# Four graph layers on one core: softmax scores spread by a DRAM round trip, with a new order of the work

## The chip, the core and the metric

The kernel runs on one core of a Trainium2 chip. A core has a matrix engine, TensorE (PE in the profile; PEld is its loading of weights), a vector engine, VectorE (DVE), a scalar engine, ScalarE (ACT), a general engine, GpSimd (POOL), and SyncE (SP), which here issues every DMA. Each engine runs its own instructions strictly in order and waits on semaphores. SBUF is the on-chip memory of 128 partitions; PSUM is the memory that matmuls write, here used as 8 banks of 128 x 512 floats.

The metric is the device time in microseconds (us) of one launch that handles all 64 graphs.

## The reference

64 graphs of 256 nodes with 512 features go through four layers. Each layer normalizes the features, applies relu, and adds the layer's result to the features:

```python
h = jnp.maximum(_layernorm(x, axis=-1), 0.0)
x = x + _L0_gnn_ref(h, adj, L0_gnn_W_qk, L0_gnn_W_v)
```

Layers 1 (attention with 8 heads, masked by the adjacency) and 2 (8 heads, tanh of masked scores) are not touched except in their place in time. Layers 0 and 3 give each node one score and take a softmax over the 256 nodes of its graph. Layer 0:

```python
scores = jnp.einsum('bnd,bmd->bnm', q, k) * inv_scale
w = jnp.sum(scores * adj_matrix, axis=-1, keepdims=True)
w = jax.nn.softmax(w, axis=1)
return w * v
```

Layer 3 does the same with other projections: `w` from `q` and `adj @ k`, a softmax over nodes, then `w * v`. Everything is float32.

## The kernel before

**Tiling.** Every tile has 128 partitions; a graph's 256 nodes are two nodes per partition (`c` = 0, 1). A loop over 64 graphs (b) is written out whole. The work of one graph is cut into 150 named steps, each a function that issues a few instructions, nearly always on one engine. A name ends in its layer or part:

- `load` (SP): features, adjacency, and the adjacency once more as 32 x 32 blocks (tile `blocks`). `at` (DVE) transposes the blocks; `neg`, `negt` (ACT) make additive masks.
- per layer: `st` (DVE statistics), `rs` (DVE), `pw` (POOL, power -0.5), `sh` (DVE, shift), `hn` (ACT, normalized relu), `sq` (DVE, block transposes), `sw` (SP, store to a DRAM tile `sq_d`), `ht` (SP, four reads that complete the transposition). PE multiplies `ht` with weights.
- layer 0: `qk` and `qe` (PE, ACT), `score0` (PE), `s0v` (DVE: one score per node, tile `wc`, 128 x 2).
- layer 1: `fa`, `fb` (PE projections), `fae`, `fbe` (DVE), `send`, `er`, `enes` (per-node terms to DRAM and back to all partitions, 2 MB), `max` (DVE), `mxv`, `mxt`, `mr`, `mb` (maxima to DRAM and back to all partitions, 1 MB), `ea`, `ex` (ACT), `eg`, `eh` (POOL), `eb` (DVE), `po`, `su`, `sp` (PE), `se`, `oe` (ACT), `sr` (DVE), `sqo`, `swo`, `or`, `oa` (result through DRAM, then POOL adds it).
- layer 2: `xp`, `xe`, `sqx`, `swx`, `xpt`, `xc`, `xcv`, `xca`, `ps`, `tv`, `ta`, `py`, `ye`, `sqy`, `swy`, `yr`, `yg`, `yv`.
- layer 3: `agg`, `ga`, `z`, `zv` (scores into `wc`), `am`.
- the softmax over nodes, in layers 0 and 3, built by `weighted`: `pv` (PE, the values), `softp` (PE), `softv` (DVE, maximum), `softa` (ACT, exponentials and their sum), `softw` (DVE, weights of the node pairs), `add` (DVE, adds weighted values to the features). `store` (SP) ends the graph.

`softp` is the step that the change replaces. Each partition holds two scores, but the maximum and the sum run over all 256. Two PE transposes of a broadcast column (line 751 in the profile) put all 256 scores on every partition, in a PSUM bank. Line 756 is `softv`, 761 and 763 are `softa`, 768 and 769 `softw`, 775 `add`.

**Order.** Nothing schedules at run time. Tables give every step a number: `WEIGHTS` for set-up, `FIRST` for the first six graphs, `LAST` for the last five, `TIMES` for all others, and graph b's numbers are shifted by b times `PERIOD`. All steps of all graphs are sorted by that number, and the five engines' instructions are pinned in the sorted order:

```python
steps += [(b * PERIOD + at, b, name) for name, at in times.items()]
```

So up to five graphs are in flight, and each engine takes turns among them. The numbers are keys for sorting; no engine waits for a clock.

**Buffers.** `keep(kind, count, ...)` makes a fixed number of tiles of a kind. `take` pops the oldest free one, `done` gives it back, both in the sorted order, so the order also decides who waits for whose buffer. Every DMA is issued by SP, in order: a step whose wait isn't over holds up all DMAs behind it.

**Lines used below.** 639 is every projection from `ht` (`qk`, `pv`, `fa`, `fb`, `xp`, `z`); 650 the `ht` reads; 733 the `sq_d` stores; 706 `sh`; 701 `pw`; 942 `eg`; 966 `po`; 896 `max`; 1149 `yg` and `yv`; 645 `sq`.

## Time and profile before

| What | Value |
|---|---|
| median of 3 runs | 3910.57 us (3908.46 to 3915.72) |
| time of the profiled execution | 3894.62 us |
| its span, first to last instruction | 3892.8 us |
| instructions in the span | 52870 |
| matmuls of the removed step (line 751) | 256, 53.4 us busy |
| all DMA | 784.71 MB, mean 202 GB/s |
| share of 16 DMA engines' span, data queue | 63.8% |

The page gives for each engine its busy time, its share of the span and its number of instructions. A stretch is a part of the span, with the same per engine. A wait line names the waiting engine and line, what it waited for, the total in us, how often, and the longest. A group line gives busy time, mean length of one in ns, and the engine's idle time ahead of it. A timeline line gives start, length, engine, line, operation, and in brackets the idle time before it and what ended it. The chain is followed back from the last instruction through whatever released each step.

### The profile page before, as it was taken

The numbers are of one execution on the slowest core, as the hardware profiler recorded it, in microseconds if no ns is written. First come the engines' busy times: TensorE is split into PE (matmuls) and PEld (weight loads), VectorE is DVE, ScalarE is ACT, GpSimd is POOL, SyncE is SP. The second block draws the span as 40 slices with busy tenths as digits, with TensorE's granted clock in tenths as the row PEclk, the third lists the DMA queues.
The fourth block names the chain that finished last, engine by engine and source line by source line (L and its number), as shares of the span: only waits on it lengthen the run. The fifth ranks groups of instructions, "written<-read, shape, count | busy, mean of one in ns | idle before, by whom it ended". The sixth has DMA issues, their size and how long they took to land.

```text
span 3892.8 us, 52870 instructions
## 1 busy us (share of the span) xinstructions
PE 3677.6 (94%) x16322; PEld 2126.0 (55%) x16322; DVE 3060.4 (79%) x7449; ACT 1872.2 (48%) x3653; POOL 1531.4 (39%) x1229
## 2 busy tenths in 40 slices
PE   6789999999999999999999999999999999999889
PEld 3455555555555555555555555555555555555544
DVE  5777787887888787787787787887788787787784
ACT  2444554545545544545544544545545544544442
POOL 1434343444344344343344344343344344344341
PEclk9899999999999999999999999999999999999999
DMA  7565666666666666666666666666666666666553
GB/s 200 168 193 179 208 200 212 214 203 213 216 201 211 217 200 212 207 199 207 215 195 213 207 202 214 214 204 209 216 201 216 214 198 215 209 200 196 181 182 103
DMA packets 967435, 784.71 MB, mean 202 GB/s; under 512 B 788913, under 2 KB 859121, under 8 KB 942577
## 3 DMA queue, kind: packets, MB, share of 16 engines
q1 hardware_dynamic: 967152, 781.34, 63.8%
q8 instruction: 130, 2.13, 0.2%
q14 instruction: 153, 1.25, 0.1%
HBM read 511.12 MB, written 270.01 MB: 201 GB/s over the span
## 4 chain that ended last, share of the span: by engine, by line
PE 46%; DVE 20%; DMA 17%; SPq 8%; issue 5%; POOL 3%; ACT 2%; DVEq 0%; ACTq 0%; POOLq 0%
PE bank L639 34%; DVE sq L645 7%; DMA ht<-sq_d 6%; SPq L650 5%; DMA sq_d<-sq 5%; PE bank L1111 4%; PE bank L966 3%; DVE pair L948 2%; DVE junk L896 2%; DMA hn<-sq_d 2%; PE bank L1097 2%; DVE stats L690 2%; DMA blocks<-in_adj_dram 2%; DVE xt L775 2%; DVE shift L706 1%
## 5 line engine op out<-in xcount | busy, mean ns | idle before, releaser
L639 PE MATMUL bank<-w_s,ht 128*128 128x256 f32 (+2 forms) x3072 | 965.7, 462 | 80.7 <-DMA ht<-sq_d 69.0
L639 PE MATMUL bank<-wv_s,ht 128*128 128x512 f32 x2048 | 906.3, 594 | 0.0
L639 PEld LDWEIGHTS bank<-w_s,ht 128*128 128x128 f32 x3072 | 587.4, 198 | 381.3 <-issue 288.2
L713 ACT ACTIVATE hn<-xt,shift,rstd 128x512 f32<-128x512 f32 x512 | 388.7, 806 | 828.8 <-DVE shift L706 759.5
L942 POOL TENSOR_TENSOR pair<-pair,negt 128x1024 f32<-128x1024 f32 x256 | 604.5, 2374 | 117.2 <-ACT pair L935 117.2
L639 PEld LDWEIGHTS bank<-wv_s,ht 128*128 128x128 f32 x2048 | 397.3, 197 | 444.8 <-issue 442.8
L975 POOL TENSOR_TENSOR half<-pair 128x512 f32<-128x512 f32 x256 | 331.3, 1306 | 593.1 <-PE bank L989 328.0
L896 DVE CUSTOM_DVE_ANT_0 junk<-all,adj 128x256 f32<-128x256 f32 x1024 | 472.8, 462 | 31.4 <-issue 0.2
L639 PE MATMUL bank<-m_s,ht 128*128 128x512 f32 x1024 | 455.5, 597 | 8.2 <-DMA ht<-sq_d 6.8
L935 ACT ACTIVATE pair<-all,ec 128x256 f32<-128x256 f32 x1024 | 433.4, 497 | 9.8 <-DMA all<-er_d 9.8
L1149 POOL TENSOR_TENSOR xt<-xt,hn 128x512 f32<-128x512 f32 x64 | 111.4, 1741 | 811.7 <-DMA hn<-sq_d 811.7
L690 DVE BATCH_NORM_STATS2 stats<-xt 128x6 f32<-128x512 f32 x512 | 332.3, 680 | 96.3 <-POOL xt L1034 88.5
L701 POOL TENSOR_TENSOR rstd<-rstd,power 128x2 f32<-128x2 f32 x256 | 179.5, 702 | 407.0 <-DVE rstd L697 390.9
L645 DVE STREAM_TRANSPOSE sq<-hn 128x512 f32<-128x512 f32 x512 | 331.8, 686 | 5.0 <-ACT hn L713 4.9
L966 PE MATMUL bank<-pair,feats 128*64 128x256 f32 x2048 | 272.4, 401 | 62.2 <-ACT pair L954 62.0
L1129 DVE TENSOR_TENSOR pair<-bank,at 128x512 f32<-128x512 f32 x512 | 317.0, 669 | 12.2 <-PE bank L1097 12.0
L954 ACT ACTIVATE pair<-pair 128x1024 f32<-128x1024 f32 x256 | 264.0, 1050 | 118.4 <-DVE pair L948 111.2
L639 PEld LDWEIGHTS bank<-m_s,ht 128*128 128x128 f32 x1024 | 197.2, 198 | 221.4 <-issue 216.4
L948 DVE TENSOR_TENSOR pair<-pair,all 128x1024 f32<-128x1024 f32 x256 | 303.4, 1223 | 15.3 <-DMA all<-m_d 14.4
L1032 POOL TENSOR_TENSOR hn<-hn,rs 128x256 f32<-128x256 f32 x256 | 152.3, 617 | 392.4 <-DMA hn<-sq_d 317.7
L761 ACT ACTIVATE bank<-bank,nmax 128x256 f32<-128x256 f32 x128 | 56.8, 443 | 504.5 <-DVE nmax L756 504.5
L1136 ACT ACTIVATE pair<-pair 128x512 f32<-128x512 f32 x512 | 285.8, 617 | 16.1 <-DVE pair L1129 16.0
(83 smaller groups left out, 4541.8 us busy)
## 6 DMA issues: line engine op xcount, KB each, us to landing
sq_d<-sq SPq DMA_DIRECT2D x448, 512.0 KB
ht<-sq_d SPq DMA_DIRECT2D x1024, 128.0 KB
all<-er_d SPq DMA_DIRECT2D x128, 1024.0 KB
all<-m_d SPq DMA_DIRECT2D x64, 1024.0 KB
hn<-sq_d SPq DMA_DIRECT2D x512, 128.0 KB
xt<-in_x_dram SPq DMA_DIRECT2D x64, 512.0 KB
xpt<-sq_d SPq DMA_DIRECT2D x256, 128.0 KB
out_dram<-xt SPq DMA_DIRECT2D x64, 512.0 KB
```

What stands on the lines that cost most here:

```text
L639: nc.tensor.matmul(p, chunk(ht[:, k], c), w[:, k], start=(k == 0), stop=(k == KC - 1))
L645: nc.vector.transpose(sq.rearrange("p (r k i c) -> p c k r i", r=4, k=KC, c=NC)[:, c], t[:, c])
L690: nc.vector.bn_stats(stats[:, c, :], g["xt"][:, c, :])
L713: nc.scalar.activation(hn[:, c, :], g["xt"][:, c, :], AF.Relu, bias=st["shift"][:, c:c + 1], scale=st["rstd"][:, c:c + 1])
L896: nc.vector.tensor_tensor_reduce(junk, g["en"][:, h, :], g["adj"][:, c, :], 1.0, -BIG, OP.add, OP.max, g["mx"][:, c, h:h + 1])
L935: nc.scalar.activation(e[:, s, j, :], g["es"][:, h, :], AF.Prelu, bias=st["ec"][:, j, H + h:H + h + 1], alpha=0.2)
L942: nc.gpsimd.tensor_tensor(e, e, g["negt"][:, None].to_broadcast([P, 2, NC, N]), OP.add)
L948: nc.vector.tensor_tensor(e, e, g["m"][:, 2 * p:2 * p + 2, None, :].to_broadcast([P, 2, NC, N]), OP.subtract)
L966: nc.tensor.matmul(po[s * U:(s + 1) * U, p % 2, :], feats[:, j, h * U:(h + 1) * U], e[:, s, j, :], start=(j == 0), stop=(j == NC - 1))
L975: nc.gpsimd.tensor_tensor(g.take("half", name=f"h{p}"), e[:, :, 0, :], e[:, :, 1, :], OP.add)
L1129: nc.vector.tensor_tensor(th[:, s], g[f"ps{p}{s}"].rearrange("p (m n) -> p m n", m=NC), g["at"], OP.mult)
L1136: nc.scalar.activation(g[f"th{p}"][:, s], g[f"th{p}"][:, s], AF.Tanh)
```

## The change

The step `softp` goes. In its place stand `ws`, which stores the 128 x 2 scores to a DRAM tile `w_d`, and `wb`, which reads them back as one row of 256 to all 128 partitions, into an SBUF tile of a new kind `pr` (two of them). `softv` and `softa` then read that SBUF tile and no PSUM bank. The kind `blocks` has one tile in place of two. In the set-up the names of two banks get the number of their part. All tables have new numbers, and `PERIOD` is 57.0; 152 steps a graph.

```diff
@@ -471,13 +473,14 @@
     keep("hn", 2, [P, NC, D])
     keep("ht", 3, [P, KC, N])
     keep("sq", 2, [P, NC * D])
-    keep("blocks", 2, [P, N // S, S * NC])
+    keep("blocks", 1, [P, N // S, S * NC])
     keep("feats", 2, [P, NC, D])
     keep("cols", 2, [P, KC, N])
     keep("all", 3, [P, H, N])
     keep("pair", 4, [P, 2, NC, N])
     keep("negt", 2, [P, NC, N])
     keep("qk", 2, [P, NC, 2 * A0])
+    keep("pr", 2, [P, N])
     keep("mx", 1, [P, NC, S])
     keep("half", 2, [P, 2, N])
 
@@ -594,7 +597,7 @@
             @step(f"mt{e}")
             def _():
                 for s in range(2):
-                    pt = g.take("bank", name=f"wt{s}")
+                    pt = g.take("bank", name=f"wt{s}{e}")
                     for k in range(KC):
                         nc.tensor.transpose(pt[:, k * P:(k + 1) * P], st[f"wn{e}"][:, s, k], ident)
 
@@ -602,10 +605,10 @@
             def _():
                 st["w_t"] = w_t = once.tile([P, 2, D], F32, name="w_t", bufs=1)
                 nc.vector.tensor_copy(w_t[:, 0, :].rearrange("p (k d r) -> p k d r", k=KC, r=4),
-                                      g["wt0"].rearrange("p (k r d) -> p k d r", k=KC, r=4))
-                nc.vector.tensor_copy(w_t[:, 1, :], g["wt1"])
-                g.done("wt0")
-                g.done("wt1")
+                                      g[f"wt0{e}"].rearrange("p (k r d) -> p k d r", k=KC, r=4))
+                nc.vector.tensor_copy(w_t[:, 1, :], g[f"wt1{e}"])
+                g.done(f"wt0{e}")
+                g.done(f"wt1{e}")
 
             @step(f"mm{e}")
             def _():
@@ -744,21 +747,24 @@
                 value(c)
 
 
-            @step(f"softp{layer}")
-            def _():
-                pr = g.take("bank", name="pr")
-                for c in range(NC):
-                    nc.tensor.transpose(pr[:, c * P:(c + 1) * P], st["wc"][:, c:c + 1].to_broadcast([P, P]), ident)
+            @step(f"ws{layer}")
+            def _():
+                st["w_d"] = rows_d.tile([P, NC], F32, name="w_d")
+                nc.sync.dma_start(st["w_d"], st["wc"])
+
+            @step(f"wb{layer}")
+            def _():
+                nc.sync.dma_start(g.take("pr"), st["w_d"].rearrange("p c -> (p c)").partition_broadcast(P))
 
             @step(f"softv{layer}")
             def _():
                 st["nmax"] = small.tile([P, 1], F32, name="nmax")
-                nc.vector.tensor_reduce(st["nmax"], g["pr"][:, :N], AX.X, OP.max, negate=True)
+                nc.vector.tensor_reduce(st["nmax"], g["pr"], AX.X, OP.max, negate=True)
 
             @step(f"softa{layer}")
             def _():
                 st["tot"] = small.tile([P, 1], F32, name="tot")
-                nc.scalar.activation(g["pr"][:, :N], g["pr"][:, :N], AF.Exp, bias=st["nmax"], accum_out=st["tot"])
+                nc.scalar.activation(g["pr"], g["pr"], AF.Exp, bias=st["nmax"], accum_out=st["tot"])
                 st["w"] = small.tile([P, NC], F32, name="w")
                 nc.scalar.activation(st["w"], st["wc"], AF.Exp, bias=st["nmax"])
                 g.done("pr")
```

The tables of the middle graphs, old and new (`WEIGHTS`, `FIRST` and `LAST` are changed as thoroughly):

```diff
-PERIOD = 59.0
+PERIOD = 57.0
 TIMES = {
-    "load": 0.000, "st0": 8.598, "at": 14.291, "rs0": 17.770, "pw0": 18.151, "sh0": 19.827, "hn0": 20.197,
-    "sq0": 22.027, "neg": 23.076, "sw0": 23.619, "ht0": 26.810, "negt": 33.560, "qk0": 36.920, "qk1": 37.838,
-    "qe0": 38.562, "qe1": 39.097, "score0": 39.117, "s0v": 42.489, "softp0": 45.404, "softv0": 48.091,
-    "softa0": 48.731, "pv00": 49.189, "softw0": 52.829, "pv01": 53.476, "add0": 56.587, "st1": 58.282,
-    "rs1": 60.040, "pw1": 60.420, "sh1": 61.401, "hn1": 61.771, "sq1": 63.601, "sw1": 65.193, "ht1": 68.384,
-    "fa1": 73.209, "fa0": 75.198, "fae0": 77.504, "fae1": 78.257, "send": 79.376, "er": 79.818, "enes": 83.628,
-    "max0": 93.041, "ea0": 93.130, "ea1": 95.760, "max2": 97.616, "fb0": 97.757, "max1": 97.783, "max3": 99.552,
-    "mxv": 102.131, "mxt": 103.746, "ea2": 104.173, "mr": 104.189, "eg1": 105.093, "mb": 107.595, "ea3": 108.549,
-    "eg0": 108.704, "eb0": 112.651, "eb1": 113.945, "ex0": 114.332, "eg2": 115.240, "ex1": 115.461, "eh1": 117.705,
-    "fb1": 118.902, "fbe0": 119.237, "eg3": 120.587, "fbe1": 121.996, "po0": 122.625, "po1": 123.961,
-    "eb2": 124.009, "ex2": 125.487, "eb3": 125.789, "eh0": 126.598, "ex3": 126.782, "po2": 127.022, "oe0": 127.910,
-    "su0": 128.127, "po3": 128.638, "eh3": 128.740, "oe1": 129.974, "eh2": 130.055, "sqo": 130.841, "su1": 131.698,
-    "se": 132.525, "swo": 132.976, "or": 132.996, "sp": 136.188, "sr": 138.013, "oa0": 139.860, "oa1": 142.480,
-    "st2": 145.314, "rs2": 147.072, "pw2": 147.452, "sh2": 148.433, "hn2": 148.803, "sq2": 150.633, "sw2": 152.225,
-    "ht2": 155.416, "xp0": 159.864, "xp1": 163.649, "xe0": 166.754, "xe1": 167.673, "sqx": 168.592, "swx": 171.012,
-    "xpt": 174.204, "xc": 179.698, "xcv": 181.830, "ps0": 183.981, "tv0": 187.172, "xca": 187.563, "ps1": 188.658,
-    "ta0": 189.627, "tv3": 192.016, "tv1": 193.393, "tv2": 197.635, "ta1": 198.812, "ta3": 200.645, "ta2": 201.909,
-    "py0": 202.513, "ye0": 202.533, "py1": 204.554, "ye1": 206.911, "sqy": 207.777, "swy": 211.577, "am": 212.932,
-    "yr": 217.212, "yv": 221.001, "yg": 221.746, "st3": 223.517, "rs3": 225.557, "pw3": 225.938, "sh3": 230.347,
-    "hn3": 230.717, "agg1": 233.270, "agg0": 235.086, "sq3": 238.587, "sw3": 240.179, "ga0": 241.452,
-    "ga1": 242.287, "ht3": 248.180, "z0": 254.433, "z1": 257.973, "zv0": 258.289, "zv1": 261.830,
-    "softp3": 265.594, "pv31": 265.839, "softv3": 268.089, "softa3": 268.742, "pv30": 269.380, "softw3": 274.098,
-    "add3": 280.909, "store": 282.605,
+    "load": 0.000, "st0": 0.020, "rs0": 0.040, "pw0": 0.060, "sh0": 0.447, "hn0": 0.467, "at": 3.235, "sq0": 4.046,
+    "neg": 5.196, "sw0": 7.794, "ht0": 17.081, "negt": 24.877, "qk1": 25.097, "qk0": 25.928, "qe0": 26.481,
+    "pv01": 26.487, "qe1": 26.501, "score0": 26.521, "s0v": 30.777, "ws0": 30.797, "wb0": 34.828, "softv0": 36.256,
+    "softa0": 36.276, "pv00": 41.031, "softw0": 42.595, "add0": 46.118, "st1": 47.198, "rs1": 47.218,
+    "pw1": 47.238, "sh1": 48.261, "hn1": 48.281, "sq1": 50.408, "sw1": 57.622, "ht1": 58.705, "fa0": 58.725,
+    "fae0": 61.292, "fa1": 62.955, "fae1": 64.080, "send": 64.100, "er": 65.670, "enes": 68.954, "max0": 78.054,
+    "max2": 80.041, "max1": 80.835, "ea2": 81.782, "max3": 81.811, "ea0": 82.877, "mxv": 86.226, "mxt": 87.431,
+    "fb1": 87.694, "mr": 88.442, "fbe1": 92.928, "mb": 92.952, "ea1": 93.137, "eg0": 97.342, "eg2": 97.898,
+    "eb2": 99.758, "fb0": 101.023, "eg1": 102.751, "ex2": 103.007, "fbe0": 104.462, "ea3": 105.281, "eb0": 106.770,
+    "po2": 107.965, "ex0": 109.416, "eg3": 110.046, "po0": 110.200, "eb1": 110.242, "ex1": 110.262, "eb3": 112.539,
+    "ex3": 112.559, "eh0": 112.721, "po1": 113.101, "po3": 113.362, "oe0": 113.726, "oe1": 113.772, "eh1": 114.964,
+    "su0": 114.984, "sqo": 116.823, "swo": 116.843, "or": 116.985, "eh2": 121.455, "eh3": 121.545, "su1": 121.565,
+    "se": 121.585, "sp": 124.333, "sr": 124.353, "oa1": 127.236, "oa0": 132.559, "st2": 132.579, "rs2": 132.599,
+    "pw2": 132.619, "sh2": 133.501, "hn2": 135.131, "sq2": 135.151, "sw2": 137.255, "ht2": 140.479, "xp0": 146.490,
+    "xp1": 148.494, "xe0": 150.546, "xe1": 153.892, "sqx": 155.064, "swx": 156.419, "xpt": 161.348, "xc": 167.559,
+    "xcv": 170.132, "ps0": 171.632, "tv1": 175.365, "xca": 177.302, "ps1": 179.802, "ta1": 179.832, "tv0": 180.487,
+    "tv2": 182.563, "ta0": 182.818, "py0": 182.838, "ta2": 182.910, "tv3": 184.557, "ta3": 184.577, "am": 184.723,
+    "ye0": 185.950, "py1": 187.683, "ye1": 187.703, "sqy": 190.038, "swy": 190.249, "yr": 195.562, "yv": 200.772,
+    "yg": 202.748, "st3": 203.788, "rs3": 205.029, "pw3": 205.049, "sh3": 206.251, "hn3": 206.271, "sq3": 210.021,
+    "sw3": 210.041, "agg1": 212.553, "ht3": 213.760, "agg0": 218.026, "ga0": 222.008, "z0": 223.305,
+    "zv0": 228.215, "ga1": 229.617, "z1": 239.253, "zv1": 242.471, "ws3": 243.288, "pv30": 245.126, "wb3": 249.737,
+    "pv31": 252.572, "softv3": 255.150, "softa3": 256.059, "softw3": 260.763, "add3": 262.405, "store": 266.901,
 }
```

Sorted, the new order of the middle graphs is, from one `load` to the next (steps of several graphs in flight):

- PE: ps0, su0, fa0, fa1, su1, ps1, sp, z1, py0, py1, pv30, pv31, qk1, qk0, pv01, score0, fb1, xp0, xp1, pv00, agg1, fb0, agg0, po2, z0, po0, xc, po1, po3.
- DVE: st0, rs0, zv0, sh0, sqo, at, sq0, fae0, tv1, fae1, send, tv0, sr, tv2, tv3, zv1, st2, rs2, sqy, sh2, max0, sq2, max2, max1, max3, softv3, mxv, yv, mxt, s0v, softw3, st3, rs3, add3, sh3, fbe1, softv0, xe0, sq3, xe1, sqx, softw0, eb2, add0, st1, rs1, fbe0, sh1, eb0, sq1, eb1, eb3.
- POOL: pw0, eh1, eh2, eh3, oa1, oa0, pw2, yg, pw3, eg0, eg2, eg1, pw1, eg3, eh0.
- SP: load, sw1, ht1, swo, or, sw0, er, enes, ws3, ht0, swy, wb3, sw2, yr, ht2, ws0, mr, wb0, mb, store, sw3, swx, ht3, xpt.

## The prediction

> **What bounds the kernel now.** I read the page's busy shares first, then the chain that ended last (its part 4), then the waits of TensorE.
>
> ```profile
> PE 3677.6 (94%) x16322; PEld 2126.0 (55%) x16322; DVE 3060.4 (79%) x7449; ACT 1872.2 (48%) x3653; POOL 1531.4 (39%) x1229
> ...
> PE 46%; DVE 20%; DMA 17%; SPq 8%; issue 5%; POOL 3%; ACT 2%; DVEq 0%; ACTq 0%; POOLq 0%
> ```
>
> TensorE (PE) is nearly full, yet under half of the chain is PE: the rest goes through VectorE (DVE) and DMA round trips that finish just in time. The stretches give the size of the leftover:
>
> ```profile
> 400.00:800.00 400.00, 388.21 (x1743) 224.53 (x1742) 319.75 (x799) 201.00 (x395) 160.85 (x129) 1.00 0.66 207
> 800.00:1600.00 800.00, 777.27 (x3525) 453.54 (x3524) 645.30 (x1605) 401.69 (x788) 323.56 (x261) 1.00 0.67 210
> 1600.00:2400.00 800.00, 768.84 (x3462) 447.11 (x3461) 640.29 (x1567) 394.54 (x768) 327.39 (x259) 1.00 0.65 206
> 2400.00:3200.00 800.00, 780.62 (x3508) 453.03 (x3506) 647.15 (x1607) 404.31 (x792) 330.48 (x264) 1.00 0.66 210
> ```
>
> The first pair of numbers after the length is PE busy. A graph has 254 PE instructions, so these 2800 us hold 12238/254 = 48.2 graphs: 58.1 us each, PE busy 56.35, idle 1.77. What that idle waits for:
>
> ```profile
> PE bank L639 <- DMA ht<-sq_d: 94.6, 87, 12.4
> PE bank L966 <- ACT pair L954: 62.0, 57, 8.8
> ```
>
> Projections wait for transposed activations from DRAM; `po` waits for the exponentials. Why these are late is seen in the timeline of one graph (start, length, engine):
>
> ```profile
> 1910.85 0.70 POOL L701 TENSOR_TENSOR rstd<-rstd,power 128x2 f32<-128x2 f32 x1 [0.42 <-DVE rstd L697]
> ...
> 1911.52 2.35 POOL L942 TENSOR_TENSOR pair<-pair,negt 128x1024 f32<-128x1024 f32 x1
> 1911.59 2.30 DVE L706 SCALAR_TENSOR_TENSOR shift<-mv,rstd 128x2 f32<-128x2 f32 x1 [0.49 <-POOL rstd L701]
> ```
>
> A tiny `sh1` takes 2.30 us because GpSimd (POOL) starts `eg3` just before it; elsewhere it takes 0.16.
>
> **What the skill says.** (1) "SBUF — State Buffer", section on the two sides: DVE and GpSimd share a port pair as an exclusive lock for a whole instruction, taken also by a DVE operation with two SBUF inputs. The lines above agree: 2.30 against 0.16. (2) "DMA: Bandwidth & Descriptors", anatomy of one DMA: a fixed cost of about 2.0 us, mostly the receipt of the write. The trace agrees: its chain has a 512 KB `sq_d<-sq` at 2.64 us and `ht<-sq_d` at 2.79. (3) Same page, specifications: pieces under 512 B are below line rate. The new store has 8-byte pieces; no row of before shows them. (4) "Perfetto Trace Analysis", most-contended engine: matmul busy share misleads, as matmuls are pipelined. So I price PE by spacing of starts.
>
> **The change, part by part.** Durations below are from start to next start in the middle graphs' timelines.
>
> Removed: two transposes in each of two softmaxes. In
>
> ```profile
> 2056.74 0.43 PE L751 MATMUL bank<-ident,wc 128*128 128x128 f32 x2
> 2057.01 4.46 PE L639 MATMUL bank<-wv_s,ht 128*128 128x512 f32 x10
> ```
>
> a pair holds PE for 0.27 us, in the other layer 0.22: 0.49 per graph. The group's busy time gives an upper end, 53.4/64 = 0.83. I take 0.49 (31 us in 64 graphs); PE's floor is 56.35 - 0.49 = 55.86 per graph.
>
> Added: `ws` and `wb`, twice per graph. Each issue costs SP 0.35 us (like `sw`), 1.4 per graph; SP issues about 24 us of work per graph, so it has room, but it waits in order. Landing: `ws` 2 to 4 us (nearest: `er_d<-er` 1.8 to 2.7, `sq_d<-sq` 2.6, by semaphore updates in the trace), `wb` about 2.8 (like a 128 KB `ht` piece). So one `ws`+`wb` trip is 5 to 7 us in place of 0.5. Layer 0: its user add0 wants pv00, which PE ends 12 us after score0 (fb1, xp0, xp1, pv00: 1.73+3.52+3.44+3.43), so PE hides it; but DVE is in order, and between s0v and softv0 it has only softw3 to fbe1, 5.4 us in the loop below. At 6.1 (0.35+2.6+0.35+2.8) softv0 stands 0.7 late, of which 0.5 reaches xe1; bounds 0 and 2. Behind `wb0` on SP wait `mb`, then store; `mb` has m_d's own landing to wait for anyway. Layer 3: `ws3` stands between `enes` and `ht0` and waits for zv1; behind it `ht0`, `swy`, `wb3`. Counted from the start F of fa0: z1 ends at F+10.0, zv1 10.8, `ht0` issued 11.2 to 14.1, its last piece landing 5.9 later by the same place of before (behind the 2 MB `enes`): 19.3. qk1 wants it at 20.4. Hidden, slack 1.1. `wb3` lands near 20, softv3 stands at 24: slack 4.
>
> softv and softa read SBUF instead of PSUM: no row shows it; PSUM costs 0.39 and 0.45 us, I take no difference (0.1 either way, on engines with room). Two bank uses per graph go, 0 to a small gain. One `blocks` tile less: `load` of a graph now follows `at` of the previous by 135 steps, almost a period; nothing, and 3 us of SP per graph if `at` ran that late. The `wt` names only rename set-up banks: nothing.
>
> Moved: the whole order, the main term. The tightest loop of the new order, from F to the next F:
> - PE fa0, fa1, su1, ps1, sp, z1, py0, py1: 1.83+1.92+0.57+1.94+0.23+3.44+1.78+1.83 = 13.6 with the end of the last; ye1 0.65: 14.3.
> - DVE sqy 1.17, sh2 0.08, max0 1.71, sq2 1.21: 18.5. Then max2, max1, max3, softv3 5.8: 24.3. Meanwhile `swy` lands at 19.2 and `yr` at 23.8, POOL runs `yg` 1.75 to 25.6, and mxv (two SBUF inputs) is locked out until then.
> - mxv, yv, mxt, s0v, softw3, st3, rs3: 0.75+0.61+0.16+0.54+0.40+1.41+0.15 = 4.0: 29.6. pw3 0.75, then `eg0` starts at once, 2.35: sh3 locked until 32.7 (add3 runs beside).
> - hn3 and sq3's second half 2.3: 35.1. xe1 wants xp1, which PE ends at 35.4: 36.0. sqx, softw0, eb2, add0, st1, rs1: 2.07+0.40+1.13+1.32+1.41+0.15 = 6.5: 42.5.
> - pw1 0.75, `eg3` locks sh1 2.35: 45.6. hn1's half and eb0: 46.9; sq1 1.21: 48.1. `sw1` and `ht1` to fa0: 7.85 in before (8.35 in the graph shown): 55.9 to 56.4, or 56.9 with the 0.5 of softv0.
>
> So loop and PE floor lie within 1 us, near 56; three lock stalls (1.3, 1.8, 2.2) are inside. po0 wants ex0 about 0.4 after PE is there. Before has three such near-ties (fa1 0.32, xp0 0.66, po2 0.57 idle, medians) and so 1.77 idle. In the new order I count fa0, po0 and qk1, each at 0.3 to 0.5: idle 1.1, period 57.0. Saving 1.1 per graph; 54 graphs are steady (3130 us between 400 and 3530): 60 us. Filling: `ws0`/`wb0` of the first graphs hold SP while weights wait behind, 5 us lost, between -10 and +20; the end has pv31 of 61 and both pv of 63 (10.3 us) over the last trip, nothing. Sum -55. The profiled run took 3894.6 with a span of 3892.8; the median 3910.57 is 16 higher for the same work, so I put the difference on the median: 3856.
>
> **Rivals.**
> R1, the waits vanish: period 55.9 to 56.3, saving 97 to 119, time 3795 to 3815. For: loop and floor are nearly equal. Against: in the steady stretch before never ran below 57.4, with idle 0.9 to 1.1 even then.
> R2, the gain is eaten by the three locks and by landings behind `load`: `sw1` is issued 1.3 us after `load` instead of 4.4, so its 2.6 us may become 3.5. PE idle 2.0 to 2.4, time 3890 to 3920.
> R3, slower: `ws3` at the head of SP. It is in order, so if zv1 or the landing behind `enes` is late, `ht0` is, and qk1 stalls PE, each us in full. Slack is 1.1, the gain before it is 2.25 (58.11 - 55.86): beyond 3.3 us later than reckoned the kernel is slower. At 4 to 5 late it is +0.7 to +1.7 per graph, +40 to +90: about 3970. For: `hn` and `ht` waits are already PE's largest, and `ht0` lands at 6.6 instead of 2.8 when behind `enes`. Against: zv1 has its input at 10.0 and DVE is free by 9.2.
>
> **How the numbers follow.** The main case (3835 to 3880) gets 0.45; R1 0.17; R2 0.18, half of it faster and a third the same; R3 0.20. About 0.2% (8 us) is what a measurement can tell from no change. Faster: 0.45+0.17+0.09 = 0.71, as 0.70; same 0.06; slower 0.24. The range leaves out the lower end of R1 and most of R3: 3797 to 3930.
>
> **What would show it.** Right: no L751; PE busy near 55.9 per graph and period near 57; sh1 and sh3 at about 2 us; mxv late behind `yg`; softv waiting nowhere long for a DMA. Wrong: a large wait of DVE softv for `pr<-w_d`, or of PE qk for `ht<-sq_d` with SP held at the w_d store (R3); PE idle over 2 with fa0 waiting (R2); filling longer than 20 us more. It would also be wrong if DVE and POOL meet in other pairs than those named.

## The result, and the profile after

The changed kernel takes 4137.55 us (median of 4, 4134.67 to 4145.81) against 3913.14 (3908.46 to 3916.34) for the kernel before, measured together: a ratio of 1.0578, 95% interval 1.0557 to 1.0599. I had said 3856 with a range of 3797 to 3930. The sign is wrong and the time is far outside. The profiled executions say the same: 4134.67 against 3894.62.

The page of the changed kernel, part 1 (busy time, share of the span, instructions):

```profile
PE 3752.1 (91%) x16066; PEld 2107.1 (51%) x16066; DVE 3196.0 (77%) x7449; ACT 1906.5 (46%) x3653; POOL 1544.0 (37%) x1229
```

The 256 transposes are gone (16322 to 16066 instructions), and yet PE is busy for longer and has a smaller share of a longer span. The stretches of the changed kernel, with the columns as before:

```profile
400.00:800.00 400.00, 365.07 (x1503) 203.81 (x1502) 302.12 (x717) 179.04 (x347) 138.76 (x111) 0.97 0.69 193
800.00:1600.00 800.00, 758.95 (x3309) 427.33 (x3307) 651.23 (x1519) 392.01 (x749) 316.35 (x250) 0.98 0.73 203
1600.00:2400.00 800.00, 744.36 (x3230) 418.70 (x3226) 641.38 (x1508) 385.16 (x739) 311.73 (x247) 0.99 0.73 201
2400.00:3200.00 800.00, 742.06 (x3214) 416.12 (x3210) 634.71 (x1496) 380.89 (x734) 308.80 (x245) 0.99 0.73 199
```

A graph now has 250 PE instructions, so 11256/250 = 45.0 graphs in 2800 us: 62.2 us each, PE busy 2610.4/45.0 = 58.0, idle 4.2. Before it was 58.1, 56.35 and 1.77; I had forecast 57.0 with 1.1 idle. (A stretch doesn't hold whole graphs, so this count is good to some 0.3 us. Taken from `fa0` to `fa0` over graphs 15 to 50, counted from 0, the changed kernel has 61.7 with 57.7 busy and before 58.3 with 56.5.) The waits of the changed kernel, over all engines (engine, line, tile, what it waited for, total us, times, longest):

```profile
DVE nmax L762 <- DMA pr<-w_d: 230.4, 74, 11.7
...
PE bank L642 <- DMA ht<-sq_d: 145.2, 109, 6.8
...
PE bank L972 <- DVE feats L871: 94.3, 50, 2.7
```

Line 762 is `softv` (756 before): DVE stands 230 us for the score rows, a wait that did not exist. Line 642 is the projections (639 before): 145 against 94.6. Line 972 is `po` (966 before): it no longer waits mostly for exponentials but for `feats`, which DVE writes in `fbe0`, a step that stands behind `softv0` in DVE's order.

Where they come from is seen in one graph. SP's timeline of the changed kernel (start, length, line, DMA, how many), from `ws0` to `ht3`:

```profile
2000.20 0.34 SPq L753 DMA_DIRECT2D w_d<-wc  x1
2000.59 1.34 SPq L928 DMA_DIRECT2D m_d<-mr  x4
2003.00 0.34 SPq L757 DMA_DIRECT2D pr<-w_d  x1
2003.80 0.34 SPq L932 DMA_DIRECT2D all<-m_d  x1
2004.23 0.38 SPq L1206 DMA_DIRECT2D out_dram<-xt  x1
2011.07 2.93 SPq L736 DMA_DIRECT2D sq_d<-sq  x2
2014.10 2.76 SPq L653 DMA_DIRECT2D ht<-sq_d  x4
```

`ws0` waits for the score and goes out at 2000.20, and `mr` (m_d<-mr) goes out behind it. `wb0` needs `ws0` landed and goes out at 2003.00. `mb` (all<-m_d, 1 MB) needs `m_d` landed as well, and goes out at 2003.80, with `store` behind it. In the waits of SP, `wb` (line 757) stands long, but `mb` (line 932) still has to wait behind it:

```profile
SPq L757 <- DMA w_d<-wc: 202.5, 119, 4.6
...
SPq L932 <- DMA m_d<-mr: 27.1, 40, 2.7
```

The same stretch on DVE:

```profile
2003.54 1.89 DVE L709 SCALAR_TENSOR_TENSOR shift<-mv,rstd 128x2 f32<-128x2 f32 x1
2005.35 0.41 DVE L871 TENSOR_TENSOR feats<-bank,b_bc 128x256 f32<-128x256 f32 x1
2008.81 0.42 DVE L762 TENSOR_REDUCE nmax<-pr 128x1 f32<-128x256 f32 x1 [3.05 <-DMA pr<-w_d]
...
2018.90 2.29 DVE L709 SCALAR_TENSOR_TENSOR shift<-mv,rstd 128x2 f32<-128x2 f32 x1 [0.49 <-POOL rstd L704]
```

`softv0` waits 3.05 us for the row and everything behind it on DVE waits too. On PE the same graph and the next `fa0` (the group with 272 columns):

```profile
1971.28 3.91 PE L642 MATMUL bank<-w_s,ht 128*128 128x272 f32 x16
...
2018.56 1.08 PE L972 MATMUL bank<-pair,feats 128*64 128x256 f32 x8 [1.42 <-DVE feats L871]
...
2034.35 5.50 PE L642 MATMUL bank<-w_s,ht 128*128 128x272 f32 x16 [2.69 <-DMA ht<-sq_d]
```

From one `fa0` to the next it is 63.1 us. PE waits 1.42 for `fbe0` and 2.69 for `ht1`, and after the second wait the same 16 matmuls take 5.50 instead of 3.91: the clock record has PE at half clock from 2034.15 to 2037.57.

### The profile page after: what moved, and what is told of

Read it like the earlier page. It is cut to its first block, busy times and chain, and to the rows that moved or that the text cites. A ratio compares the mean times of both kernels' runs of the same rounds, so it can differ in the third digit from the quotient of the medians.

```text
span 4132.9 us, 53405 instructions
## 1 busy us (share of the span) xinstructions
PE 3752.1 (91%) x16066; PEld 2107.1 (51%) x16066; DVE 3196.0 (77%) x7449; ACT 1906.5 (46%) x3653; POOL 1544.0 (37%) x1229
## 3 DMA queue, kind: packets, MB, share of 16 engines
q1 hardware_dynamic: 1004016, 798.26, 69.4%
## 5 line engine op out<-in xcount | busy, mean ns | idle before, releaser
L642 PE MATMUL bank<-wv_s,ht 128*128 128x512 f32 x2048 | 922.6, 598 | 6.5 <-DMA ht<-sq_d 4.9
L642 PEld LDWEIGHTS bank<-w_s,ht 128*128 128x128 f32 x3072 | 598.0, 200 | 457.2 <-issue 323.2
L642 PE MATMUL bank<-m_s,ht 128*128 128x512 f32 x1024 | 501.8, 637 | 26.6 <-DMA ht<-sq_d 21.1
L902 DVE CUSTOM_DVE_ANT_0 junk<-all,adj 128x256 f32<-128x256 f32 x1024 | 456.9, 446 | 32.8 <-DMA all<-er_d 1.5
L981 POOL TENSOR_TENSOR half<-pair 128x512 f32<-128x512 f32 x256 | 342.3, 1349 | 330.8 <-ACT pair L960 201.7
L954 DVE TENSOR_TENSOR pair<-pair,all 128x1024 f32<-128x1024 f32 x256 | 367.4, 1456 | 1.8 <-POOL pair L948 1.0
L709 DVE SCALAR_TENSOR_TENSOR shift<-mv,rstd 128x2 f32<-128x2 f32 x256 | 326.4, 1275 | 51.1 <-POOL rstd L704 46.9
L1142 ACT ACTIVATE pair<-pair 128x512 f32<-128x512 f32 x512 | 295.7, 626 | 59.4 <-DVE pair L1135 59.2
```

What stands on the lines that cost most here:

```text
L642: nc.tensor.matmul(p, chunk(ht[:, k], c), w[:, k], start=(k == 0), stop=(k == KC - 1))
L709: nc.vector.scalar_tensor_tensor(st["shift"], st["mv"][:, :, 0], -1.0, st["rstd"], op0=OP.mult, op1=OP.mult)
L902: nc.vector.tensor_tensor_reduce(junk, g["en"][:, h, :], g["adj"][:, c, :], 1.0, -BIG, OP.add, OP.max, g["mx"][:, c, h:h + 1])
L954: nc.vector.tensor_tensor(e, e, g["m"][:, 2 * p:2 * p + 2, None, :].to_broadcast([P, 2, NC, N]), OP.subtract)
L981: nc.gpsimd.tensor_tensor(g.take("half", name=f"h{p}"), e[:, :, 0, :], e[:, :, 1, :], OP.add)
L1142: nc.scalar.activation(g[f"th{p}"][:, s], g[f"th{p}"][:, s], AF.Tanh)
```

## The experiments

Three explanations stood against each other at the start: the new order itself is bad; the row lands late and DVE stands for it; or the trip disturbs SP's queue and the big transfers behind it. The first row of the table is the mean over the 35 graphs from 15 to 50 (graphs are counted from 0). The others are medians over graphs 20 to 49, in us after the start of an `fa0`, of the steps that follow it in time; these belong to the graphs ahead of it and behind it. Landings are from the semaphore updates in the trace and good to 0.1 or 0.2 us. "e1" is the new order with the transposes on PE; the other kernels are told below. Line numbers differ a little from kernel to kernel: projections are at 631 to 642, `po` at 958 to 983, `softv` at 748 to 762.

| | e1 | after | e4 | f3 | f4 | f2 | g2 | h1 |
|---|---|---|---|---|---|---|---|---|
| from `fa0` to `fa0` | 57.9 | 61.7 | 62.7 | 61.2 | 57.7 | 60.4 | 61.8 | 58.7 |
| `s0v` ends | 28.2 | 28.9 | 30.0 | 29.1 | 28.2 | 28.2 | 28.2 | 28.2 |
| `wb0` issued | - | 32.2 | 33.2 | 32.1 | 28.6 | 31.2 | 32.4 | 32.1 |
| row landed | - | 37.7 | 38.7 | 37.5 | 31.7 | 36.7 | 38.0 | 38.0 |
| `softv0` starts | 33.5 | 37.7 | 38.7 | 34.6 | 33.5 | 36.7 | 38.0 | 38.8 |
| `mr` issued | 27.2 | 29.3 | 30.4 | 29.6 | 27.2 | 28.6 | 27.3 | 27.2 |
| `mb` issued | 29.5 | 33.1 | 34.1 | 33.1 | 29.5 | 32.0 | 29.6 | 29.6 |
| `mb` landed | 34.7 | 40.4 | 41.5 | 40.6 | 35.4 | 39.2 | 36.7 | 36.8 |
| `store` issued | 31.5 | 33.6 | 34.5 | 33.7 | 31.5 | 32.4 | 31.5 | 31.5 |
| `sw3` issued | 35.8 | 40.0 | 37.5 | 37.0 | 35.8 | 38.9 | 40.3 | 35.7 |
| `sw3` landed | 38.4 | 43.0 | 43.9 | 43.1 | 38.7 | 41.8 | 42.9 | 40.0 |
| `ht1` landed | 57.6 | 61.4 | 62.6 | 61.0 | 57.4 | 60.2 | 61.5 | 58.1 |

**e1: the new order with the old softmax.** All tables and the single `blocks` tile stay; `ws` and `wb` go out and `softp` comes back, at `wb`'s place (in the middle graphs of layer 0 just before `softv0`). One exponential of one of the last graphs moves by a few places. Here and below, `...` marks lines left out of a diff.

```diff
-    keep("pr", 2, [P, N])
...
-    "s0v": 30.777, "ws0": 30.797, "wb0": 34.828, "softv0": 36.256,
+    "s0v": 30.777, "softp0": 34.480, "softv0": 36.256,
...
-            @step(f"ws{layer}")
...
-            @step(f"wb{layer}")
...
+            @step(f"softp{layer}")
```

> The new order is kept, with two transposes on TensorE in place of the store and the read through DRAM (in the middle graphs of layer 0 between xp0 and xp1; one exponential of one late graph is moved by a few places to have a bank). Round-trip theory (the loss is VectorE standing at softv until the broadcast read lands, 3.1 us a graph, and what follows from it): the wait is gone, period 58 to 59 us in place of 62.2, time 3900 to 3970. Order theory (the loss is in where the other DMAs stand: swy behind the 2 MB broadcast, sw1 behind load): the period stays above 61, time 4080 or more.

Measured: 3886.52 us, ratio 0.995 (0.9931 to 0.9968): 0.5% under before, far under the changed kernel, and below the 3900 to 3970 that I expected. Its stretches, and its largest wait of PE:

```profile
800.00:1600.00 800.00, 789.84 (x3535) 449.32 (x3534) 689.19 (x1613) 409.26 (x789) 328.63 (x264) 1.00 0.69 210
1600.00:2400.00 800.00, 783.80 (x3499) 445.58 (x3498) 688.88 (x1570) 407.12 (x782) 329.88 (x264) 1.00 0.69 208
2400.00:3200.00 800.00, 785.55 (x3479) 446.86 (x3478) 690.21 (x1602) 406.44 (x785) 328.06 (x259) 1.00 0.69 209
```

```profile
PE bank L631 <- DMA ht<-sq_d: 86.8, 41, 25.4
```

With the stretch from 400 (x1688, 385.85) these are 12201/254 = 48.0 graphs: 58.3 each, busy 57.1, idle 1.14. From `fa0` to `fa0` it is 57.9, with 57.05 busy and 0.9 idle. The order is not to blame, and the trip by DRAM costs 6.3% of before's time (1.0578 - 0.995), some 246 us. By the starts of `fa0` in the timelines of the profiled executions, the changed kernel loses 243 us on e1: 11 up to graph 5, 47 from there to graph 15, 132 from 15 to 50 (35 graphs at 61.7 and 57.9 us) and 53 after that. It is a loss of every graph, not one of filling.

**e3: the old order with the trip.** The tables of before, `wb` at `softp`'s key and `ws` just behind the scores. SBUF has no room for row tiles beside two `blocks` tiles, so `blocks` stays at one and `pr` has one tile; one early `at` moves ahead.

```diff
-    "s0v": 42.489, "softp0": 45.404, "softv0": 48.091,
+    "s0v": 42.489, "ws0": 42.492, "wb0": 45.404, "softv0": 48.091,
...
-    keep("blocks", 2, [P, N // S, S * NC])
+    keep("blocks", 1, [P, N // S, S * NC])
...
+    keep("pr", 1, [P, N])
```

> The order of before, with the store right after the scores and the read where the transposes stood; one row tile of 1 KB, one blocks tile, and one early at moved ahead so that this fits. Round-trip theory: between s0v and softv0 the old order has 5.6 us, between zv1 and softv3 5.4, and a trip takes 9 or more, behind the 2 MB broadcast in layer 3; VectorE stands 3 us in one and 3 to 6 in the other, period 62 to 66, time 4100 to 4350. Order theory: the old order hides it, time below 3960.

Measured: 4500.24 us, ratio 1.1525 (1.1488 to 1.1562), beyond the 4100 to 4350 that I expected. In its waits:

```profile
DVE nmax L754 <- DMA pr<-w_d: 566.9, 124, 11.0
```

In the old order VectorE stands much longer for the rows. With the new one the trip costs less than half of this. The single tiles are part of this run, so it is no pure price of the trip.

**e2: eight rows.** The store writes eight copies of the row, each read by 16 partitions, so that the broadcast doesn't draw on one kilobyte.

```diff
-                st["w_d"] = rows_d.tile([P, NC], F32, name="w_d")
-                nc.sync.dma_start(st["w_d"], st["wc"])
+                st["w_d"] = rows_d.tile([8, N], F32, name="w_d")
+                nc.sync.dma_start(st["w_d"].rearrange("r (p c) -> p r c", c=NC),
+                                  st["wc"][:, None, :].to_broadcast([P, 8, NC]))
...
+                nc.sync.dma_start(g.take("pr"), st["w_d"].partition_broadcast(P // 8))
```

> As the changed kernel, but the scores are stored as eight equal rows and each of the eight is read by 16 partitions. One-row theory (the read lands after 5.6 us since 128 reads of the same 1 KB get in each other's way: its packets take 170 to 370 ns each where 56 is usual for 1 KB elsewhere): packets under 100 ns, landing near 3 us, VectorE's wait for the row falls from 230 us to under 80, time near 4000. If the read is late because of what lies ahead of it in the queues: packets and landing as they were, time within 15 us of 4137.

Measured: 4134.83 us, ratio 1.0584 (1.0564 to 1.0604), the same as the change. The read did get faster: `wb0` lands 2.5 us after its issue instead of 5.5, its packets took some 60 ns instead of 340. But the store has 1024 pieces of 8 bytes, and `ws0` lands 4.6 us after issue (29.5 to 34.1) instead of 3.2. `softv0` starts at 36.7, one us earlier, while `wb0` waits longer at the head of SP: `mb` goes out at 35.0 instead of 33.1. A us gained on one path and two lost on the other brought nothing; the time is the one that I expected if the read stayed late, though the read did not.

**e4: softv0 later.** Two keys of the middle graphs: `softv0` goes behind `sqx` in DVE's order, so that nothing stands behind the late row.

```diff
-    "wb0": 34.828, "softv0": 36.256, "softa0": 36.276,
+    "wb0": 34.828, "softv0": 40.500, "softa0": 40.600,
```

> As the changed kernel, but in the middle graphs softv0 and softa0 stand after xe1 and not before xe0. Nothing is added or removed. Round-trip theory: the 3.1 us in which VectorE stands at softv0 are filled by xe0, sq3 and xe1; VectorE's wait for the row falls under 80 us, period 59 to 60.5, time 3970 to 4050. Order theory: within 20 us of 4137.

Measured: 4147.39 us, ratio 1.0621 (1.059 to 1.0652): no gain, where I had expected 3970 to 4050. Its waits show that the edit did what it meant to, and what took its place:

```profile
PE bank L634 <- DMA ht<-sq_d: 268.1, 140, 7.4
...
DVE nmax L754 <- DMA pr<-w_d: 71.7, 42, 11.0
```

DVE's wait falls from 230.4 to 71.7, PE's wait for `fbe0` is no longer among its largest, and PE's wait for `ht` grows from 145.2 to 268.1. In the table `sw3` is issued 2.5 us earlier than in the changed kernel and still lands later, 6.4 us after its issue instead of 3.0. So a second path, through the DMA queues, was as late as the first.

**f1 and f2: one layer's trip alone.** From e1, `ws` and `wb` only in layer 3 (f1) or only in layer 0 (f2), the other layer on PE. The diff is f1's.

```diff
+            if str(layer) in "0":
+                @step(f"softp{layer}")
...
+            if str(layer) in "3":
+                @step(f"ws{layer}")
...
+                @step(f"wb{layer}")
```

> The new order; the softmax of layer 0 by transposes on TensorE, that of layer 3 by the trip through DRAM. Queue theory (wb0 stands at the head of SP's queue until ws0 has landed, so mb and store go out 3.6 us later, and behind the slow 128 KB broadcast they are still in flight when sw3 is issued; sw3, ht3, load, sw1, ht1 and so fa0 are late): layer 0 does the harm, this is within 60 us of the 3887 of both on TensorE. Wait theory (VectorE standing at a softv): softv3 never stood, so also within 30 us of 3887. A time above 4000 says that layer 3's trip, behind the 2 MB broadcast, does the harm.

> The other way round: layer 3 on TensorE, layer 0 through DRAM. Queue theory and wait theory: 4050 to 4130, nearly all of the loss. If it is below 3980, the loss is layer 3's or needs both.

Measured: f1 3952.37 us, 1.0121 (1.0087 to 1.0155), 1.7% over e1; f2 4041.78, 1.0357 (1.0327 to 1.0386), 4.1% over e1. Together 5.8 of the 6.3%. Layer 0 carries most of it. Both lie a little outside of what I expected: f1 is 66 us over e1 where I had 60 at most, and f2 is just under 4050. In the changed kernel, in layer 3, `ws3` at the head of SP lets `ht0` out at 11.7 instead of 10.5, `wb3` waits until 18.7, and `yr` begins at 22.0 instead of 20.6 (f2, without a trip in layer 3: 20.0); so `s0v` ends at 28.9 instead of 28.2.

**f3: a trip that nobody waits for.** Both softmaxes on PE as in e1; `ws` and `wb` are issued by SP as in the changed kernel, and no step reads the row.

```diff
+                @step(f"softp{layer}")
...
+                    pr = g.take("bank", name="pp")
...
+                return g["pp"][:, :N] if str(layer) in "03" else g["pr"]
...
-                nc.vector.tensor_reduce(st["nmax"], g["pr"], AX.X, OP.max, negate=True)
+                nc.vector.tensor_reduce(st["nmax"], scores_row(), AX.X, OP.max, negate=True)
```

> Both softmaxes by transposes on TensorE, and yet the scores are stored and read back as in the changed kernel, into a tile that no one reads. No engine waits for this trip; SP and the DMA queues carry all of it. Queue theory: 4050 to 4150, as the changed kernel. Wait theory: within 30 us of 3887.

Measured: 4105.65 us, ratio 1.0513 (1.0469 to 1.0557), 5.6% over e1. Nearly the whole loss appears although DVE waits for no row. PE's waits in it:

```profile
PE bank L641 <- DMA ht<-sq_d: 248.6, 125, 26.0
PE bank L983 <- ACT pair L971: 13.9, 10, 3.1
```

PE's wait for `ht` is 248.6 where e1 has 86.8; the wait for `fbe0` is gone. The table shows the path: `ws0` holds SP until the score is there, so `mr` goes out 2.4 us later than in e1; `mb` and `store` (1.5 MB together) go out 3.6 and 2.2 us later, `mb` takes 7.3 us to land instead of 5.2, and when `sw3` is issued at 37.0 they are still under way. `sw3` lands 6.1 us after issue instead of 2.6, then `ht3`, `load`, `sw1` and `ht1` are all 3 to 4 us late and `fa0` with them.

**f4: the read without the store.** From f3, `ws` goes, and `wb` reads a row of the graph's adjacency, which has long been in DRAM.

```diff
-                    nc.sync.dma_start(g.take("pr"), st["w_d"].rearrange("p c -> (p c)").partition_broadcast(P))
+                    nc.sync.dma_start(g.take("pr"), adj[b][0].partition_broadcast(P))
```

> Both softmaxes by transposes on TensorE; no store; the read stands where wb stood but takes one 1 KB row of the adjacency, so SP waits for nothing there, and no one reads the tile. If the harm comes from SP standing at wb until ws has landed: 3890 to 3950. If it comes from the broadcast holding the DMA engines (128 packets of one row at 170 to 370 ns): 4000 to 4100.

Measured: 3897.9 us, ratio 0.9978 (0.9969 to 0.9987), 0.3% over e1. The same 128 KB in the same place cost some 11 us when SP needn't wait for a landing and the row isn't fresh: the read lands 3.1 us after issue (28.6 to 31.7), near the 2.8 that I had assumed, and its packets took some 65 ns.

**g3: a trip with an old row.** From f3, `wb` reads the row that the graph before stored.

```diff
+                    row = rows_before.get(layer, st["w_d"])
+                    rows_before[layer] = st["w_d"]
-                    nc.sync.dma_start(g.take("pr"), st["w_d"].rearrange("p c -> (p c)").partition_broadcast(P))
+                    nc.sync.dma_start(g.take("pr"), row.rearrange("p c -> (p c)").partition_broadcast(P))
```

> Both softmaxes on TensorE, an unused trip issued by SP as in the kernel that took 4106; but wb reads the row that the graph before had stored, so SP stands at ws for the scores and no longer at wb for the landing of ws. If the landing of ws at the head of SP's queue is the cost: 3890 to 3950. If ws's own place is, or the packets of the broadcast: 4020 to 4106.

Measured: 4025.11 us, ratio 1.0316 (1.0269 to 1.0362): 3.7% over e1, where f3 has 5.6. `wb0` doesn't wait for its store and its packets took some 57 ns, but `ws0` still waits for `s0v` ahead of `mr`, so `mr` goes out 1.4 and `mb` 2.8 us later than in e1, and `sw3` lands at 41.6. Since f4's reads alone cost 0.3%, it is the stores, at this place of SP, that are dear. It also shows that `wb0`'s wait for `ws0`'s landing is not what holds `mb`: from the issue of `ws0` to that of `mb` it is 3.7 us here without this wait, 3.6 in f3 and 3.9 in the changed kernel with it. `mb` waits for `m_d`. With `ws0` just ahead of `mr` on SP it goes out 3.2 to 3.5 us after `mr` (the changed kernel, f2, f3, g3), in e1, f1 and f4 2.3 us. Why `m_d` then lands later stays open. What f3 loses beyond g3 isn't taken apart: its score is 0.9 us later and its `mb` takes 7.3 us instead of 6.3.

**g1 and g2: the trip issued by ScalarE.** g1 is the changed kernel, g2 is f2, with `ws` and `wb` on ScalarE.

```diff
-                nc.sync.dma_start(st["w_d"], st["wc"])
+                nc.scalar.dma_start(st["w_d"], st["wc"])
...
-                nc.sync.dma_start(g.take("pr"), st["w_d"].rearrange("p c -> (p c)").partition_broadcast(P))
+                nc.scalar.dma_start(g.take("pr"), st["w_d"].rearrange("p c -> (p c)").partition_broadcast(P))
```

> As the changed kernel, but ws and wb of both layers are issued by ScalarE and no longer by SP. In layer 0 ScalarE has 8 idle us around them. If SP standing at ws and wb is what costs, SP's order is again that of the kernel without the trip: 3880 to 3960, with VectorE perhaps still 1 to 3 us late at softv0. If it is the DMA traffic of the trip itself: 4080 or more.

> Layer 3 by transposes on TensorE, layer 0 by the trip, issued by ScalarE. Against 4042 with the same trip issued by SP: 3870 to 3920 if SP's standing is the cost, 4000 to 4050 if the late row at VectorE is.

Measured: g1 4158.2 us, 1.0667 (1.0643 to 1.0692); g2 4109.98, 1.0543 (1.0515 to 1.0571), against 1.0357 for f2 and above both ranges that I had put down. The Trainium skill, "DMA: Bandwidth & Descriptors", section "Issuing engines are not separate DMA queues", says that DMAs of all engines run on the same 16 DMA engines and that issuing from another saves only the sequencer's time. In g2 that time was there to be saved: `mb` goes out at 29.6 as in e1, 3.5 us before the changed kernel's. The time of the kernel got no better, since the row now lands at 38.0, 1.3 us later than in f2, and `softv0` starts with it: `ws0` takes 4.0 us to land instead of 2.9, and the row's first packet starts 3.5 us after the issue of `wb0` instead of 1.4, with `mb` under way ahead of it. g2's waits:

```profile
PE bank L974 <- DVE feats L873: 156.5, 51, 4.7
...
DVE nmax L762 <- DMA pr<-w_d: 248.0, 59, 8.1
```

With SP's path mended the other remains, and is longer; PE's loss is a wait for `fbe0` behind `softv0`, the mirror image of f3. In g1 ScalarE also stands at `wb3`, `ea2` starts at 19.9 instead of 17.5, and `mb` goes out at 32.7 all the same.

**g4: e1 with an earlier load.** To see whether room in the queues can be bought, `load` of the middle graphs goes right behind `store`; graphs 6 to 11 keep the old keys.

```diff
-    "load": 0.000, "st0": 0.020,
+    "load": -18.000, "st0": 0.020,
```

> The new order with transposes on TensorE (3887), and in the middle graphs load issued right after store, where SP stands some 4 us for sq3, in place of just ahead of sw1. sw1 should land 2.6 us after issue in place of 3.6 and fa0 should no longer wait its 0.5 us: 3850 to 3880. If TensorE, 98 % busy, is all that counts: 3880 to 3890.

Measured: 3967.56 us, ratio 1.0177 (1.015 to 1.0204), 2.3% over e1, against what I expected. `load` is issued at 36.0, ahead of `sw3`, which now goes out at 38.9 instead of 35.8 and lands at 43.0 instead of 38.4. So a late `sw3` costs time with no trip in the kernel at all; of its 4.6 us, 3.1 are its later issue behind `load`'s and 1.5 its slower landing.

**h1: both paths at once.** From g2, three keys of the middle graphs move `softv0` behind `sqx` and `softw0` behind `eb2`. Layer 3 is on PE, layer 0 makes its trip from ScalarE.

```diff
-    "pv01": 26.487, "qe1": 26.501, "score0": 26.521, "s0v": 30.777, "ws0": 30.797, "wb0": 34.828, "softv0": 36.256,
-    "softa0": 36.276, "pv00": 41.031, "softw0": 42.595, "add0": 46.118, "st1": 47.198, "rs1": 47.218, "pw1": 47.238,
...
+    "pv01": 26.487, "qe1": 26.501, "score0": 26.521, "s0v": 30.777, "ws0": 30.797, "wb0": 34.828, "pv00": 41.031,
+    "softv0": 41.500, "softa0": 41.600, "softw0": 42.900, "add0": 46.118, "st1": 47.198, "rs1": 47.218,
```

> Layer 3 on TensorE, layer 0 by the trip issued by ScalarE (4110 with VectorE's order unchanged), and in the middle graphs softv0 stands after sqx and softw0 after eb2, so that VectorE has work until the row lands. This takes away both paths at once: SP's queue is free of the trip and VectorE is not held by it. Two-path theory (each path alone is late enough to set the period, so that taking one away gained nothing): 3870 to 3930. If a third thing is at work, such as the traffic of the trip or ScalarE's standing: above 4000.

Measured: 3959.86 us, ratio 1.0141 (1.0102 to 1.018). Two of its stretches and its PE waits:

```profile
800.00:1600.00 800.00, 781.72 (x3446) 445.15 (x3445) 693.49 (x1593) 405.77 (x780) 327.68 (x259) 1.00 0.72 209
1600.00:2400.00 800.00, 778.91 (x3433) 441.79 (x3432) 687.35 (x1596) 403.22 (x780) 324.15 (x259) 1.00 0.72 209
```

```profile
PE bank L632 <- DMA ht<-sq_d: 75.5, 46, 5.1
PE bank L974 <- ACT pair L962: 53.3, 57, 4.4
```

Neither wait is left: `ht` is below e1's 86.8, and `fbe0` is not among the largest. The wait for the exponentials is larger than e1's (53.3 against 20.1). The same kind of move that brought nothing in e4 brings 4.0% of before's time here, and the period falls from 61.8 to 58.7, of 57.9 in e1. Relative to g2, that is 3.1 of 3.9 us a graph. What stays, 1.9% over e1 or some 75 us, is between the two sizes that I had expected; about 0.75 us a graph of it is in the middle graphs, where `mb` still lands at 36.8 instead of 34.7 and `sw3` at 40.0 instead of 38.4 (the trip's own traffic in the queues is my reading; no run took it apart), and more than half lies ahead of graph 15 and after graph 50 (38 of 64 us between the two profiled executions), where the first and last graphs' tables still have the early `softv0`; that this is why was not tried.

## Why the prediction was wrong

**The order: right in its idle time, short in its gain.** I counted 1.1 us of idle a graph for the new order; e1 has 1.14 by the stretches and 0.9 from `fa0` to `fa0`. But I also put PE's busy time at 55.86 without the transposes, so 56.35 with them. From graph 15 to 50 e1 has 57.05 for the 254 instructions for which before has 56.45, 0.6 more. So a period of 57.0 could not have come out even without any trouble: e1 runs at 57.9 where before runs at 58.3, a saving of 0.3 where I had 1.1 (0.6 with the transposes kept). That PE's busy time moves with the order I had not allowed for; why it does stays open.

**The trip, "so one trip is 5 to 7 us", at 6.1: mis-sized.** Measured from the end of `s0v` it is 8.8 (28.9 to 37.7). The store was right in layer 0: 3.2 us in a range of 2 to 4. In layer 3, behind the 2 MB of `enes`, it took 7.5 (11.2 to 18.7). The read was wrong. "About 2.8, like a 128 KB `ht` piece" measured 5.5. That `ht` piece was the wrong neighbour; f4's bare read of 128 packets lands in 3.1, so it isn't the shape either. It is that all 128 packets read one row that had just been written (the last section has the figures). "softv0 stands 0.7 late" became 4.2 later than in e1, far outside the bounds of 0 and 2 that I had kept, and "0.5 reaches xe1" became nearly all of it, since `fbe0` stands in the same line and `po2` needs it.

**"Behind `wb0` on SP wait `mb`, then store; `mb` has m_d's own landing to wait for anyway": the step that failed.** It put the trip's cost on SP at nothing. The reason given held: `mb` does wait for `m_d`, and `wb0`'s wait adds next to nothing to it (g3). But I looked only behind `wb0`, and not behind `ws0`, which stands ahead of `mr` and waits for `s0v`. So `mr` goes out 2.1 us later than in e1 (1.4 in g3), and `m_d` needs some 1.4 us more to land; `mb` goes out at 33.1 instead of 29.5. Then it takes 7.4 us to land instead of 5.2, beside the slow read. And I didn't ask what is late next. `mb` and `store` are 1.5 MB, and moved 2 to 4 us they are under way when the smaller but urgent `sw3` is issued. f3 shows that the trips' whole cost on SP and in the queues, without any reader of the row, is 5.6% of before's time, of the 6.3; layer 3's trip is part of it. How it divides between the late issue and the slow read was not taken apart: f4 has 0.3% without a store and with an old row, g3 3.7% with the store and an old row.

**Two paths, not a sum.** I added up delays along one loop. Here two delays of nearly the same size meet again at `fa0`: the row by way of DVE (f2, g2), and the queue by way of `sw3` and `ht` (f3). Taking away either alone brought nothing or little (e4 nothing; f3, which has no reader, 0.7 of the 6.3%). g2 against f2 is a weaker case, as it took away SP's delay but made the row 1.3 us later. Taking away the second as well brought 4.0% of before's time (h1 against g2), of the 5.9% that g2 loses on e1.

**Rivals.** R3 had the sign and a cause of the right kind, a store at the head of SP, but the wrong place. `ht0` behind `ws3` lands at 20.7 instead of my 19.3, and it is felt: PE's idle time ahead of `qk` from graph 4 on is 14.2 us in all, 1.5 in e1. But these are 13 of some 245. `wb3` lands at 23.5 where I had said near 20; the slack of 4 is 0.8, and holds in 26 of the 30 graphs from 20 to 49. R2's sign, PE idle over 2 with `fa0` waiting, is there, and its `sw1` too: it lands 3.9 us after issue in the changed kernel and 3.8 in e1. It belongs to the new order and is part of what e1 has.

**Locks: right in two of three.** `sh1` takes 2.29 and `sh3` 1.89 us in the graph shown, `sh2` only 0.12, as the exclusive lock of the Trainium skill, "SBUF — State Buffer", section "SBUF: two separate sides", would have it. `sh0`, which I had not named, takes 1.22, in e1 too, so DVE and POOL meet in one more place. `mxv` wasn't locked out: `yr` came so late that `yg` started after it.

**The clock: not thought of.** PE's mean granted clock is 0.975 against 0.990. At half clock it spent 208 us of its span instead of 79; if it worked through those 129 us, they cost half, 65 us. It follows from the waits (below) and makes each of them dearer.

**The fixed 2.0 us of a DMA.** The section that point (2) of the prediction names is about DMAs that GpSimd issues; here SP issues all of them. The prediction's own lines, 2.64 us for 512 KB and 2.79 for 128 KB, don't show how much of that is fixed. The price of the trip didn't rest on it.

**Filling, and the median.** `fa0` of graph 5 starts at 336.5 us in the changed kernel and 339.5 before: within my -10 to +20. The 16 us that I added since the profiled execution of before ran below its median were no property of the work: after's is 3 below its median, e1's 5 above.

## What to carry to other kernels

On a queue that issues in order, each new DMA that waits for a result, here `ws0`, must be priced as a wait of everything behind it, and then two steps further: which landings are later for it, what big transfer goes out later, and which smaller urgent one will then be behind it. When a fix of one late path brings nothing, look at whether the consumer has a second one of the same size before dropping the theory; a run that keeps the cost but takes away the reader (f3) and one that takes away both (h1) settle it. An order and an operation that were laid out together should be measured apart: here the order alone was the better kernel.

## What the runs showed that I had not expected

**A fresh row is slow to broadcast.** In graphs 20 to 49, 128 packets of 1 KB from a row stored just before in 8-byte pieces took some 340 ns each in layer 0 (median of the graphs' means) and some 175 in layer 3. From a row one graph old they took 57 (g3), from an adjacency row 65 (f4), from eight fresh copies 62 (e2). How fresh can be read within g2 and h1, where the row's packets start at different times. In the graphs in which the first packet started 1.0 to 2.0 us after the landing of `ws0`, the mean was 212 to 400 ns; in those in which it started later than 3.3 us, 46 to 80, mostly 46 or 47. So here one row was slow to read for some 2 to 3 us after it landed. The row came no earlier for it, since in g2 and h1 it waited for `mb` instead. Over all graphs of the changed kernel the packets took 233 ns on average, an estimate that gives the kernel's other 1 KB packets e1's mean of 59: 2 x 128 x 0.233 = 60 us of DMA engine time per graph, over 64 graphs and 16 engines 239 us or 5.8% of the span. The queue's share is 69.4%; before has 63.8 and e1, with before's bytes, 66.1, so part of the rise is the order's. Why a fresh single row is slow stays open.

**The half clock goes by a grid.** The clock records change only on a grid of 3.41 us. Between 400 and 3200 us the changed kernel has 24 entries into half clock, the kernel before none and e1 two. In the changed kernel each followed a grid window in which matmuls ran for 0.21 to 0.46 of the time (in e1 0.30 and 0.41), and in these three traces no window that stayed at full clock followed one under 0.43. The Trainium skill, "TensorE: Matmul & The Clock Gate", Part 1, says that PE goes to half rate after an idle window of about 3.4 us. The length agrees; but a window needn't be idle here, under about 0.45 busy was enough. So a wait of 2 us at the wrong phase costs up to half a window, 1.7 us, more, as an estimate from these figures.

**Queues.** `sw3`, 512 KB, landed 2.6 us after issue in e1 and about 6 in f3 and e4. It is the same DMA, with `mb` and `store` a few us nearer ahead of it.
